# Attention block on one core: the first image's x split between two queues, the shift taken from rstd, and warming from a tile of zeros

## Chip, core and metric

One core of a Trainium2 chip. The metric is the device time of one launch in microseconds, median of the runs. The engines: PE (TensorE), DVE (VectorE), ACT (ScalarE), POOL (GpSimd) and SP (SyncE); SP and ACT each issue DMAs on a hardware queue of their own, POOL on a software queue.

## What is computed

A group norm over 8 groups of 64 channels, then attention with four heads of 128 channels over 1024 positions, a projection and a residual, for 16 images of 512 x 32 x 32, all in float32.

```
xg = x.reshape(b, NUM_GROUPS, -1)
xn = ((xg - mean(xg)) * rsqrt(var(xg) + EPS)).reshape(b, c, h, w)
xn = xn * norm_gamma[:, None, None] + norm_beta[:, None, None]
qkv = einsum('oc,bchw->bohw', qkv_w, xn) + qkv_b[:, None, None]
q, k, v = split(qkv, 3, axis=1)                      # 4 heads each
attn = softmax(einsum('bhnd,bhmd->bhnm', q, k) * dh ** -0.5)
out = einsum('bhnm,bhmd->bhnd', attn, v)
out = einsum('oc,bchw->bohw', proj_w, out) + proj_b[:, None, None]
return x + out
```

## The kernel before

x lies in SBUF as four chunks of 128 channels (partitions) by 1024 positions, `xs[b, c]`. An image goes through the norm, the products for v, q and k (by Strassen-like schemes of seven products or more, so that sums of blocks are formed on DVE first), scores, exponentials, the weighted sum and the projection; the next image's preparation is laid between the scores of the present one. From the first scores on PE goes from one product to the next.

The change touches only the opening of the first image. `open_image` writes out by hand what each engine does there, in program order (`pin`), with priorities (`urgent`) for the scheduler:

- `load_x(0, ...)` asks for each chunk in two column halves of 512 positions, 256 KB each: the left by SP's queue, the right by ACT's. Chunks 0 and 1 (`KC` = 2) come first, then chunks 2 and 3 between the loads of v's weights.
- `stage_v` loads v's weights in blocks `a11`, `a12`, `a21`, `a22` of 256 x 256, each in two pieces `k` of 128 KB, by `load_w`.
- `stats_on_vector(c)` takes mean and variance of chunk 0, then 1, with one BATCH_NORM_STATS2 for a column half and one aggregate. Two products with the averaging matrix `avg` carry them over the channels of a group: `pivot` (L2280, on the first half's mean alone, result `pm`) and `product` (L2300, on the deviations `e` from that pivot). `about` forms `e` from the aggregate and `pm`.
- From the second product ACT forms the variance (`power_on_scalar`), POOL its power -1/2 (`root`: `rstd`), ACT minus the mean (`minus_mean_on_scalar`: `mu`). DVE then makes `sc` = rstd x gamma (`scale`) and `sh` = mu x sc + beta (`shift`), and `quarter` normalises 256 columns at a time, on DVE or ACT. The first product for v (L1065, tile `v_x`) reads such a quarter and a11.
- Chunk 2 goes through DVE and chunk 3 through ACT (`stats_on_scalar`, tile `junk`), then as a pair through the same steps (`lower`).
- `warm(n, jj)` lays n products of `avg` by `avg`, 128 x 128, into tiles `seed`, which nobody reads before they are overwritten. One product in float32 shows as two records of PE.

The program uses eight semaphores for the DMAs of SP and ACT together, DMAHW0 to DMAHW7, in turn. A DMA that takes a semaphore waits until the earlier DMA on it has landed, and the queue behind it waits too.

Of the kernel before, what the change touches and what calls it, by code (L numbers as in the profile page):

```python
# [12 lines left out]
AF = mybir.ActivationFunctionType  # L13
# [3 lines left out]
P = 128  # L17
# [4 lines left out]
HALF = 512  # L22
# [156 lines left out]
KC = 2  # L179
# [56 lines left out]
def fast_path(ctx, tc, x, sources, out, consts, flag, dims):  # L236
# [6 lines left out]
    nc = tc.nc  # L243
    B, C, N, NCC, NH2, NB, GC, SCALE = dims
    gamma, beta, qkv_wT, qk_b, v_b, proj_wT, proj_b = sources
    avg, neghalf, gamma_sb, beta_sb, qkb_sb, vb_sb, projb_sb = consts
# [36 lines left out]
    xs, xb, vs, qs, ks, os_, ob = {}, {}, {}, {}, {}, {}, {}  # L283
# [5 lines left out]
    def load_x(b, chunks=range(NCC)):  # L289
        for c in chunks:  # L290
            if b not in xw:
                xw[b] = every_x
            xs[b, c] = xw[b][:, ts(c, N)]
            for half in range(NH2 if b == 0 else 1):
                i = ts(half, HALF) if b == 0 else ds(0, N)

                eng = nc.gpsimd if b > 0 else nc.scalar if half == 1 else nc.sync
                dma = eng.dma_start(xs[b, c][:, i], x[b, ts(c, P), i])  # L298
                if b > 0:

                    tc.keep_in_program_order(dma)


    home = {
        h: tpool.tile([P, 4, HALF], F32, tag=f"home{h}", name=f"home_{h}") for h in "AB"
    }
    load_x(0, range(KC))
    primer = one.tile([BLK, 1], F32, name="primer")
    for t, src in ((gamma_sb, gamma), (beta_sb, beta)):
        nc.gpsimd.dma_start(t, src)  # L310
    nc.gpsimd.memset(ones, 1.0)
# [260 lines left out]
    def stage_v():  # L572

        beside["v"] = vpool.tile([P, 4, HALF], F32, tag="v", name="wv")
        for i, n in enumerate(("a11", "s1", "a12", "s2")):
            wv[n] = beside["v"][:, i].rearrange("p (k m) -> p k m", m=HC)
        two = [ypool.tile([P, KC, HALF], F32, tag="y", name=f"wv_{i}") for i in range(2)]
        for i, n in enumerate(("a21", "a22", "s4")):
            wv[n] = two[i // 2][:, i % 2].rearrange("p (k m) -> p k m", m=HC)
        beside["spare"] = two[1][:, 1]  # L580
        wv["s3"] = wv["a21"]
        base = 2 * C

        def load_w(n, k, eng):
            r, kk = int(n[1]) - 1, int(n[2]) - 1
            eng.dma_start(wv[n][:, k, :], qkv_wT[ts(KC * kk + k, P), ds(base + r * HC, HC)])

        load_w("a11", 0, nc.sync)
        load_x(0, range(KC, KC + 1))
        load_w("a11", 1, nc.scalar)  # L590
        load_x(0, range(KC + 1, NCC))
        for n in ("a21", "a22", "a12"):
            for k in range(KC):
                load_w(n, k, nc.sync)

    def keep_kept(site, part, eng):

        if site == "v":

            t = rpool.tile([P, 4, HALF], F32, tag=f"r{part}", name=f"kv_tt_{part}")  # L600
            tt = t[:, :2].rearrange("p s (f d) -> p s f d", d=P)
            beside["s4"] = t[:, 2].rearrange("p (f d) -> p f d", d=P)
        else:
            tt = lpool.tile([P, 2, 4, P], F32, tag="tt", name=f"kproj_tt_{part}")
        if part == 0 and site == "proj":
            beside["s4"] = beside["spare"].rearrange("p (f d) -> p f d", d=P)
        if part == 0:
            keep_factors(
                site, ((0, (0, 1)), (1, (0, 1))),
                beside["v"].rearrange("p f (k c d) -> p f k c d", k=KC, c=2),  # L610
                (tt[:, 0], tt[:, 1], beside["s4"]), eng,
            )
            return
        for i, (n, g, o) in enumerate((("s3", 2, 0), ("a22", 2, 1), ("s4", 3, 0))):
            one = slice(i, i + 1)
            keep_factors(
                site, ((g, (o,)),),
                wv[n].rearrange("p k (c d) -> p k c d", c=2).unsqueeze(1),
                (tt[:, 0, one], tt[:, 1, one], beside["s4"][:, one]), eng,
            )  # L620
# [111 lines left out]
    shift = {"now": 0, "next": 0}  # L732
# [1506 lines left out]
    def warm(n, jj):  # L2239

        for _ in range(n):
            i = warmed[jj]
            warmed[jj] += 1
            ins = nc.tensor.matmul(  # L2244
                seeds[jj][:, ts(i % (HALF // P), P)], avg, avg,
                start=(i == 0), stop=True, skip_group_check=True,
            )
            tc.keep_in_program_order(ins)

    def open_image(units):  # L2250


        pin = tc.keep_in_program_order
        mvs[0] = gn.tile([P, NCC, 2], F32, tag="mv", name="mv_0")
        mean, var = ([mvs[0][:, c, i : i + 1] for c in range(NCC)] for i in range(2))
        act, dve = nc.scalar, nc.vector
# [4 lines left out]
        class Chain:  # L2261
# [74 lines left out]

            def minus_mean(self):
                pin(dve.tensor_sub(self.mu, self.mu, self.pms))

            def minus_mean_on_scalar(self):  # L2340
                self.mu, off = self.small("mu"), self.e[:, 0, 0:1]
# [2 lines left out]
                    self.mu, self.pm[0], AF.Identity, scale=-1.0, bias=off  # L2344
                ))

            def scale(self):
                self.sc, self.sh = self.small("sc"), self.small("sh")
                pin(dve.tensor_mul(
                    self.sc, self.rstd, gamma_sb[:, self.c[0] : self.c[-1] + 1]  # L2350
                ))

            def shift(self, i):
                c, o = self.c[i], slice(i, i + 1)
                scaled[0, c] = self.sc, self.sh, i
                pin(dve.scalar_tensor_tensor(
                    self.sh[:, o], self.mu[:, o], self.sc[:, o], beta_sb[:, c : c + 1],
                    ALU.mult, ALU.add,
                ))

        def stats_on_vector(c):
            both = gn.tile([P, NH2 + 1, 6], F32, tag="st", name=f"st_{c}")
            st = both[:, :NH2]
            steps = [
                lambda h=h: pin(dve.bn_stats(st[:, h, :], xs[0, c][:, ts(h, HALF)]))
                for h in range(NH2)
            ]
            steps.append(lambda: pin(
                dve.bn_aggr(mvs[0][:, c, :], st.rearrange("p h s -> p (h s)"))
            ))  # L2370
            return steps, both
# [24 lines left out]
        upper, lower = [Chain(c) for c in range(KC)], Chain(KC, KC + 1)  # L2396

        def urgent(step, *args):
            with tc.high_priority(URGENT):
                return step(*args)  # L2400
# [8 lines left out]
        upper[0].pivot(st[:, 0, 1:2])  # L2409
        run(steps[1:])  # L2410
        urgent(upper[0].about, 0)
        warm(2, 1)
        urgent(upper[0].product)
        warm(1, 1)
        urgent(upper[0].power_on_scalar)
        urgent(upper[0].minus_mean_on_scalar)
        steps, st = stats_on_vector(1)
        run(steps[:1])
        urgent(upper[1].pivot, st[:, 0, 1:2])
        warm(4, 1)  # L2420
        run(steps[1:])
        urgent(upper[1].about, 0)
        urgent(upper[1].product)
# [15 lines left out]
        sum_c()  # L2439
        run(steps[:1])  # L2440
        urgent(upper[1].scale)
        urgent(upper[1].shift, 0)
        quarter(1, 0)
        quarter(1, 1)
        square_c()
# [3 lines left out]
        s1, a21, a22 = wv["s1"], wv["a21"], wv["a22"]  # L2449
# [45 lines left out]
    seeds = [ps_s.tile([P, HALF], F32, tag="s", name=f"seed_{jj}") for jj in range(2)]  # L2495
# [20 lines left out]
    for s in range(steps + 1):  # L2516
        units = []
        if s < steps:
            b, h, j = where(s)
# [12 lines left out]
        for half in range(NH2):  # L2532
# [21 lines left out]
            n = (len(units) + 1) // 2  # L2554
# [158 lines left out]
```

## Time and profile before

| what | value |
|---|---|
| time, median of 3 runs | 3101.13 us (3101.08 to 3101.16) |
| the profiled execution | 3100.82 us, its span 3099.2 us |
| PE busy | 3093.6 us of the span |
| DVE, ACT, POOL busy | 2709.8, 1758.0 and 455.6 us |
| DMA | 647.70 MB, mean 209 GB/s |
| first v product starts | 9.50 us after the span's start |

Times in rows are in microseconds from the span's start. A busy PE is not PE at its peak, since matmul records overlap and their ends are modelled: the pace is read from starts. The change lies in the first 20 us; the views of that stretch are the timeline, the chain of waits and the landings of DMAs.

### The profile page before, as it was taken

Reading aid. Unit: us, or ns where it says so; the run is one execution under the profiler, and the core shown is the slowest. Engines: PE = TensorE matmul, PEld = TensorE weight load, DVE = VectorE, ACT = ScalarE, POOL = GpSimd, SP = SyncE. Lnnn points to the kernel's source line nnn. Section 1 sums busy time; section 2 is a strip of 40 time slices with the busy share of each in tenths; the row PEclk is TensorE's granted clock in tenths of the full one; section 3 lists DMA queues with packets and bytes.
Section 4 is the critical chain, followed back from the end, with each engine's and each line's share of the span. In section 5 each row is a group of like instructions: output and inputs, shape, how many; then the busy total and the mean of one; then the engine's idle time right before and its main releaser. Section 6 shows DMA issues by size and latency. Waiting matters only on the chain.

```text
span 3099.2 us, 39180 instructions
## 1 busy us (share of the span) xinstructions
PE 3093.6 (100%) x12168; PEld 2274.1 (73%) x12168; DVE 2709.8 (87%) x4870; ACT 1758.0 (57%) x3882; POOL 455.6 (15%) x763
## 2 busy tenths in 40 slices
PE   9999999999999999999999999999999999999999
PEld 7567777777777777777777777777777777777775
DVE  8989989889798897988979889898898979989787
ACT  4546556565565655656556565565655656556543
POOL 0131112111111111111111111111111101111010
PEclk9999999999999999999999999999999999999999
DMA  5597686766767667666676666767667566676751
GB/s 180 192 299 262 208 257 213 228 201 200 222 210 216 199 204 218 212 206 205 203 230 204 210 203 200 230 198 214 204 209 221 201 212 207 211 225 194 218 193 42
DMA packets 246228, 647.70 MB, mean 209 GB/s; under 512 B 32816, under 2 KB 77744, under 8 KB 246016
## 3 DMA queue, kind: packets, MB, share of 16 engines
q1 hardware_dynamic: 169248, 380.78, 40.5%
q0 software_dynamic: 63952, 229.91, 21.3%
q10 hardware_dynamic: 12816, 34.48, 3.5%
q8 instruction: 98, 1.61, 0.2%
q14 instruction: 114, 0.93, 0.1%
HBM read 468.08 MB, written 176.96 MB: 208 GB/s over the span
## 4 chain that ended last, share of the span: by engine, by line
PE 100%; DVE 0%; issue 0%
PE s L1787 28%; PE po L1886 28%; PE t_x L1332 16%; PE t_y L1332 8%; PE pp_x L829 6%; PE t_z L1332 4%; PE pp_y L829 3%; PE qk_x L829 2%; PE pp_z L829 1%; PE qk_y L829 1%; PE v_x L1065 0%; PE v_x L829 0%; PE lx L2006 0%; PE seed L2244 0%; PE qk_z L829 0%; PE v_y L829 0%
## 5 line engine op out<-in xcount | busy, mean ns | idle before, releaser
L1886 PE MATMUL po<-p,v 128*128 128x512 f32 x2048 | 1045.4, 592 | 0.0
L1787 PE MATMUL s<-qk,qk 128*128 128x512 f32 x2048 | 1045.2, 592 | 0.0
L1793 ACT ACTIVATE p<-s 128x512 f32<-128x512 f32 x1024 | 610.9, 597 | 510.5 <-PE s L1787 501.2
L1886 PEld LDWEIGHTS po<-p,v 128*128 128x128 f32 x2048 | 616.1, 301 | 375.8 <-issue 259.6
L1808 DVE TENSOR_TENSOR tot<-tot,p 128x1024 f32<-128x1024 f32 (+1 forms) x408 | 472.2, 1158 | 138.8 <-ACT p L1793 134.9
L1787 PEld LDWEIGHTS s<-qk,qk 128*128 128x128 f32 x2048 | 357.6, 189 | 44.5 <-issue 22.7
L1356 DVE TENSOR_TENSOR r<-t_y,t_u 128x342 f32<-128x342 f32 x448 | 217.2, 485 | 157.8 <-PE t_y L1332 122.7
L1452 DVE TENSOR_TENSOR r<-r,r 128x684 f32<-128x684 f32 x308 | 263.7, 864 | 1.6
L1332 PE MATMUL t_x<-home_B,w 128*128 128x171 f32 x1176 | 219.0, 308 | 0.0
L1332 PE MATMUL t_x<-home_A,w 128*128 128x171 f32 x1176 | 219.0, 308 | 0.0
L1332 PEld LDWEIGHTS t_x<-home_B,w 128*128 128x128 f32 x1176 | 188.6, 189 | 35.3 <-issue 23.4
L1332 PEld LDWEIGHTS t_x<-home_A,w 128*128 128x128 f32 x1176 | 188.6, 189 | 35.3 <-issue 23.4
L1292 ACT COPY t_u<-t_x 128x342 f32<-128x342 f32 x224 | 91.8, 410 | 138.7 <-PE t_x L1332 129.8
L1209 DVE TENSOR_TENSOR f<-x 128x684 f32<-128x684 f32 x196 | 168.0, 857 | 0.9
L1142 POOL DMA_DIRECT2D v<-vd x240 | 139.9, 590 | 148.3 <-DMA vd<-vu 58.5
L1332 PEld LDWEIGHTS t_z<-f,w 128*128 128x128 f32 x616 | 104.4, 190 | 60.5 <-issue 40.2
L298 POOL DMA_DIRECT2D x<-in_x x60 | 32.8, 551 | 718.1 <-PE t_x L1332 449.4
L1425 DVE STREAM_TRANSPOSE vu<-vt 128x128 f32<-128x128 f32 x448 | 124.2, 404 | 0.0
L1298 ACT ACTIVATE t_u<-t_x,bias 128x171 f32<-128x171 f32 x224 | 84.2, 403 | 66.3 <-PE t_x L1332 66.3
L1247 POOL DMA_DIRECT2D kept_t<-home_A x112 | 61.4, 549 | 382.0 <-DVE home_A L1240 369.6
L1332 PE MATMUL t_y<-f,w 128*128 128x171 f32 x616 | 116.8, 307 | 0.0
L1332 PE MATMUL t_z<-f,w 128*128 128x171 f32 x616 | 116.7, 308 | 0.0
(421 smaller groups left out, 4991.4 us busy)
## 6 DMA issues: line engine op xcount, KB each, us to landing
w<-kept SPq DMA_DIRECT2D x191, 512.0 KB, 3.9
w<-kept SPq DMA_DIRECT2D x191, 384.0 KB, 3.9
kept_t<-home_A POOLq DMA_DIRECT2D x112, 342.0 KB, 3.7
home_B<-kept_t SPq DMA_DIRECT2D x112, 342.0 KB, 3.4
rinv<-row ACTq DMA_DIRECT2D x63, 512.0 KB, 4.4
x<-in_x POOLq DMA_DIRECT2D x60, 512.0 KB, 6.1
v<-vd POOLq DMA_DIRECT2D x240, 128.0 KB, 4.4
out_y<-y_c POOLq DMA_DIRECT2D x60, 512.0 KB, 3.3
```

Of the source, the lines that this page charges most:

```text
L829: latest["product"] = nc.tensor.matmul(acc[:, ts(i, Q)], have["w"][t][:, i, slot, :], inner(i, bn), start=(first and i == 0), stop=True, s ...
L1142: nc.gpsimd.dma_start(vs[b, pair][ts(q, BLK), half].rearrange("m h (k i) j -> m (h k) (i j)", k=n), rows.rearrange("(k m) (q e) -> q m k e ...
L1209: (eng.tensor_add if op == "+" else eng.tensor_sub)(made[f], of(a), of(c))
L1292: nc.scalar.copy(dst, src)
L1332: latest["product"] = nc.tensor.matmul(acc[:, ts(i, H3)], wts[G, t][:, i, slot, :], moving, start=(start and i == 0), stop=True, skip_grou ...
L1356: out = nc.vector.tensor_add(dst, view(a), view(c))
L1425: nc.vector.transpose(to[:, k], of[:, k])
L1452: (nc.vector.tensor_add if add else nc.vector.tensor_sub)(at(o), a, c)
L1787: latest["score"] = nc.tensor.matmul(sc, ks[b, h][:, ts(j, P)], qs[b, h][:, ts(half, HALF)], start=True, stop=True)
L1793: exps[s] = nc.scalar.activation(ps[s][:, ts(half, HALF)], sc, AF.Exp, scale=SCALE)
L1808: added[b, h, j] = nc.vector.tensor_add(tot[b, h][:, i], tot[b, h][:, i], ps[s][:, i])
L1886: summed = nc.tensor.matmul(po[half], v_block(b, h, j), ps[s][:, i], start=(j == 0), stop=(j == NB - 1),)
```

## The change

- x's chunks 0 and 1: each column half is asked for in two parts of 64 channels, one by SP, one by ACT, so the halves follow each other on both queues. These eight DMAs take all eight semaphores.
- The second piece of a11 moves from ACT's queue to SP's, behind chunk 3's left half; a21 and a22 are asked for piece by piece instead of block by block.
- `still`, 128 x 128 zeros in `home["A"]` (a tile that is used much later), is set by POOL ahead of its first DMAs, and the warming multiplies `still` by itself instead of `avg` by `avg`. Two warming products are dropped: one ahead of chunk 0's `product`, one ahead of chunk 1's.
- The shift of chunk 0 and of the pair of chunks 2 and 3: `mu` is multiplied by gamma (ACT for chunk 0, DVE for the pair) while POOL takes the power, and `sh` = mu x rstd + beta no longer reads `sc`. Chunk 1 keeps `sc`.

```diff
--- before.py
+++ after.py
@@ -293,6 +293,11 @@
             xs[b, c] = xw[b][:, ts(c, N)]
             for half in range(NH2 if b == 0 else 1):
                 i = ts(half, HALF) if b == 0 else ds(0, N)
+                if b == 0 and c < KC:
+                    for part, eng in enumerate((nc.sync, nc.scalar)):
+                        r = ts(part, P // 2)
+                        eng.dma_start(xs[0, c][r, i], x[0, ds(c * P + part * P // 2, P // 2), i])
+                    continue
 
                 eng = nc.gpsimd if b > 0 else nc.scalar if half == 1 else nc.sync
                 dma = eng.dma_start(xs[b, c][:, i], x[b, ts(c, P), i])
@@ -306,6 +311,8 @@
     }
     load_x(0, range(KC))
     primer = one.tile([BLK, 1], F32, name="primer")
+    still = home["A"][:, 0, :P]
+    nc.gpsimd.memset(still, 0.0)
     for t, src in ((gamma_sb, gamma), (beta_sb, beta)):
         nc.gpsimd.dma_start(t, src)
     nc.gpsimd.memset(ones, 1.0)
@@ -587,11 +594,13 @@
 
         load_w("a11", 0, nc.sync)
         load_x(0, range(KC, KC + 1))
-        load_w("a11", 1, nc.scalar)
         load_x(0, range(KC + 1, NCC))
-        for n in ("a21", "a22", "a12"):
-            for k in range(KC):
+        load_w("a11", 1, nc.sync)
+        for k in range(KC):
+            for n in ("a21", "a22"):
                 load_w(n, k, nc.sync)
+        for k in range(KC):
+            load_w("a12", k, nc.sync)
 
     def keep_kept(site, part, eng):
 
@@ -2242,7 +2251,7 @@
             i = warmed[jj]
             warmed[jj] += 1
             ins = nc.tensor.matmul(
-                seeds[jj][:, ts(i % (HALF // P), P)], avg, avg,
+                seeds[jj][:, ts(i % (HALF // P), P)], still, still,
                 start=(i == 0), stop=True, skip_group_check=True,
             )
             tc.keep_in_program_order(ins)
@@ -2336,6 +2345,7 @@
 
             def minus_mean(self):
                 pin(dve.tensor_sub(self.mu, self.mu, self.pms))
+                pin(dve.tensor_mul(self.mu, self.mu, self.gammas()))
 
             def minus_mean_on_scalar(self):
                 self.mu, off = self.small("mu"), self.e[:, 0, 0:1]
@@ -2344,17 +2354,26 @@
                     self.mu, self.pm[0], AF.Identity, scale=-1.0, bias=off
                 ))
 
+            def by_gamma_on_scalar(self):
+                pin(act.activation(
+                    self.mu, self.mu, AF.Identity, scale=self.gammas()
+                ))
+
+            def gammas(self):
+                return gamma_sb[:, self.c[0] : self.c[-1] + 1]
+
             def scale(self):
                 self.sc, self.sh = self.small("sc"), self.small("sh")
                 pin(dve.tensor_mul(
-                    self.sc, self.rstd, gamma_sb[:, self.c[0] : self.c[-1] + 1]
+                    self.sc, self.rstd, self.gammas()
                 ))
 
-            def shift(self, i):
+            def shift(self, i, by=None):
                 c, o = self.c[i], slice(i, i + 1)
                 scaled[0, c] = self.sc, self.sh, i
+                by = self.rstd if by is None else by
                 pin(dve.scalar_tensor_tensor(
-                    self.sh[:, o], self.mu[:, o], self.sc[:, o], beta_sb[:, c : c + 1],
+                    self.sh[:, o], self.mu[:, o], by[:, o], beta_sb[:, c : c + 1],
                     ALU.mult, ALU.add,
                 ))
 
@@ -2409,15 +2428,16 @@
         upper[0].pivot(st[:, 0, 1:2])
         run(steps[1:])
         urgent(upper[0].about, 0)
-        warm(2, 1)
+        warm(1, 1)
         urgent(upper[0].product)
         warm(1, 1)
         urgent(upper[0].power_on_scalar)
         urgent(upper[0].minus_mean_on_scalar)
+        urgent(upper[0].by_gamma_on_scalar)
         steps, st = stats_on_vector(1)
         run(steps[:1])
         urgent(upper[1].pivot, st[:, 0, 1:2])
-        warm(4, 1)
+        warm(3, 1)
         run(steps[1:])
         urgent(upper[1].about, 0)
         urgent(upper[1].product)
@@ -2439,7 +2459,7 @@
         sum_c()
         run(steps[:1])
         urgent(upper[1].scale)
-        urgent(upper[1].shift, 0)
+        urgent(upper[1].shift, 0, upper[1].sc)
         quarter(1, 0)
         quarter(1, 1)
         square_c()
```

SP's queue from its first DMA, before (`wv` without a number holds a11 and later a12, `wv_217` a21 and a22, `st` pieces of the weights for q and k):

```order
L298 DMA x<-in_x 128x512 x2
L586 DMA wv<-in_qkv_wT 128x256
L298 DMA x<-in_x 128x512 x2
L586 DMA wv_217<-in_qkv_wT 128x256 [waits DMAHW0_49]
L586 DMA wv_217<-in_qkv_wT 128x256 [waits DMAHW2_49]
L586 DMA wv_217<-in_qkv_wT 128x256 [waits DMAHW4_49]
L586 DMA wv_217<-in_qkv_wT 128x256 [waits DMAHW5_49]
L586 DMA wv<-in_qkv_wT 128x256 [waits DMAHW6_49]
L586 DMA wv<-in_qkv_wT 128x256 [waits DMAHW7_49]
L460 DMA st_0_231<-in_qkv_wT 128x2x128 [waits DMAHW0_49]
```

and after (`wv` holds a11, `wv_222` a21 and a22):

```order
L299 DMA x<-in_x 64x512 x4
L593 DMA wv<-in_qkv_wT 128x256 [waits DMAHW0_49]
L303 DMA x<-in_x 128x512 [waits DMAHW1_49]
L303 DMA x<-in_x 128x512 [waits DMAHW2_49]
L593 DMA wv<-in_qkv_wT 128x256 [waits DMAHW4_49]
L593 DMA wv_222<-in_qkv_wT 128x256 [waits DMAHW6_49]
L593 DMA wv_222<-in_qkv_wT 128x256 [waits DMAHW7_49]
L593 DMA wv_222<-in_qkv_wT 128x256 [waits DMAHW0_49]
L593 DMA wv_222<-in_qkv_wT 128x256 [waits DMAHW1_49]
L593 DMA wv<-in_qkv_wT 128x256 [waits DMAHW2_49]
L593 DMA wv<-in_qkv_wT 128x256 [waits DMAHW3_49]
L467 DMA st_0_236<-in_qkv_wT 128x2x128 [waits DMAHW4_49]
```

Before, five DMAs go without a wait, a11 among them as the third; now four half-height ones do, and a11, the chunks 2 and 3 and the second a11 each wait for a landing. The first `st` waits for a later DMA's landing.

PE's opening, before (`seed` the warming, `pm` the two products of the statistics):

```order
L2244 MATMUL seed_242<-avg 128x128 [waits DVE_49]
L2244 MATMUL seed_242<-avg 128x128 x8
L2280 MATMUL pm_246<-st_260,avg 128x1 [waits DVE_49]
L2244 MATMUL seed_243<-avg 128x128 x2
L2300 MATMUL pm_246<-e_245,avg 128x2 [waits DVE_49]
L2244 MATMUL seed_243<-avg 128x128
L2280 MATMUL pm_248<-st_282,avg 128x1 [waits DVE_49]
L2244 MATMUL seed_243<-avg 128x128 x4
L2300 MATMUL pm_248<-e_247,avg 128x2 [waits DVE_49]
L2244 MATMUL seed_243<-avg 128x128 x2
L1065 MATMUL v_1_x<-wv,x 128x256 [waits DMAHW4_49,DMAHW1_49,DVE_49]
```

and after:

```order
L2253 MATMUL seed_247<-home_A 128x128 [waits Pool_49]
L2253 MATMUL seed_247<-home_A 128x128 x8
L2289 MATMUL pm_251<-st_265,avg 128x1 [waits DVE_49]
L2253 MATMUL seed_248<-home_A 128x128
L2309 MATMUL pm_251<-e_250,avg 128x2 [waits DVE_49]
L2253 MATMUL seed_248<-home_A 128x128
L2289 MATMUL pm_253<-st_287,avg 128x1 [waits DVE_49]
L2253 MATMUL seed_248<-home_A 128x128 x3
L2309 MATMUL pm_253<-e_252,avg 128x2 [waits DVE_49]
L2253 MATMUL seed_248<-home_A 128x128 x2
L1074 MATMUL v_1_x<-wv,x 128x256 [waits DMAHW1_49,DMAHW0_49,DVE_49]
```

The warming waits for POOL instead of DVE, one product less stands ahead of chunk 0's `pm<-e` and one less ahead of chunk 1's.

DVE from the end of chunk 1's statistics, before (`e` the deviations, `ve` chunk 1's variance):

```order
L2292 TENSOR_TENSOR e_247<-mv_244,pm_248 128x1 [waits DVE_49,PE_49]
L2293 SCALAR_TENSOR_TENSOR e_247<-e_247,mv_244 128x1 [waits DVE_49]
L2349 TENSOR_TENSOR sc_0_298<-rstd_0_277,gamma_sb 128x1 [waits DMASW0_49,Pool_49]
L2356 SCALAR_TENSOR_TENSOR sh_0_299<-mu_0_279,sc_0_298,beta_sb 128x1 [waits DMASW1_49,DVE_49,Activation_49]
L111 TENSOR_SCALAR x<-x,sc_0_298,sh_0_299 128x256 [waits DVE_49]
L2320 SCALAR_TENSOR_TENSOR ve_1_304<-pm_248,d_1_296 128x1 [waits Activation_49]
```

and after:

```order
L2301 TENSOR_TENSOR e_252<-mv_249,pm_253 128x1 [waits DVE_49,PE_49]
L2302 SCALAR_TENSOR_TENSOR e_252<-e_252,mv_249 128x1 [waits DVE_49]
L2367 TENSOR_TENSOR sc_0_302<-rstd_0_281,gamma_sb 128x1 [waits DMASW0_49,Pool_49]
L2375 SCALAR_TENSOR_TENSOR sh_0_303<-mu_0_283,rstd_0_281,beta_sb 128x1 [waits DMASW1_49,Activation_49]
L111 TENSOR_SCALAR x<-x,sc_0_302,sh_0_303 128x256 [waits DVE_49]
L2329 SCALAR_TENSOR_TENSOR ve_1_308<-pm_253,d_1_300 128x1 [waits Activation_49]
```

The order is the same (later a few sums for q and k change places on DVE); `sh` waits for ACT's `mu` and for beta, no longer for the instruction ahead of it.

## The prediction

> **What bounds the kernel now.** I read the page first (which engine, and whether it waits), then the chain of waits in order of time for the first 45 us, then the timeline of the opening, and last the views of the DMAs.
>
> ```profile
> span 3099.2 us, 39180 instructions
> ...
> PE 100%; DVE 0%; issue 0%
> ```
>
> The chain lies on PE for the whole span, so nothing that is hidden beside PE is worth anything. What can move is the time at which PE begins its useful work, and any wait before it is saturated.
>
> ```profile
> 1.64 4.21 PE seed L2244 x18
> ...
> 9.61 2.75 PE v_x L1065 x12
> ...
> 17.53 3.45 PE seed L1065 x16
> 20.98 10.36 PE v_x L1065 x48
> ```
>
> "seed L2244" is the warming, products that nobody reads. The first useful product is v_x at 9.50 (row below). From 17.53 on PE goes at its own pace: 10.36/48 = 0.216 us a record, as 3.45/16. The chain stays on PE between the two as well. So the change is worth what it moves the start at 9.50, if nothing gives it back before 17.53. The timeline of the opening:
>
> ```profile
> 0.98 0.86 SPq L298 DMA_DIRECT2D x<-in_x  x2
> 1.07 0.17 DVE L314 MEMSET avg<- 128x128 f32 x1 [1.07 <-PEq L2701]
> ...
> 1.52 0.70 POOL L310 DMA_DIRECT2D gamma_sb<-in_gamma  x1 [0.84 <-POOLq L2701]
> ...
> 2.77 0.12 POOL L311 MEMSET ones<- 32x1 f32 x1
> 2.80 0.17 POOL L320 MEMSET table<- 128x64 f32 x1
> ...
> 4.61 0.34 ACTq L586 DMA_DIRECT2D wv<-in_qkv_wT  x1
> 4.61 1.29 DVE L2365 BATCH_NORM_STATS2 st<-x 128x6 f32<-128x512 f32 x2 [3.02 <-DMA x<-in_x]
> 5.64 0.42 PE L2280 MATMUL pm<-st,avg 128*128 128x1 f32 x2
> 5.93 0.21 DVE L2369 BATCH_NORM_AGGREGATE mv<-st 128x2 f32<-128x12 f32 x1
> 6.25 0.15 DVE L2292 TENSOR_TENSOR e<-mv,pm 128x1 f32<-128x1 f32 x1
> 6.72 0.38 PE L2300 MATMUL pm<-e,avg 128*128 128x2 f32 x2
> 7.87 0.57 POOL L2327 TENSOR_TENSOR rstd<-ve,neghalf 128x1 f32<-128x1 f32 x1 [4.90 <-ACT e L2342]
> 7.88 0.26 ACT L2343 ACTIVATE mu<-pm,e 128x1 f32<-128x1 f32 x1
> 8.54 0.15 DVE L2349 TENSOR_TENSOR sc<-rstd,gamma_sb 128x1 f32<-128x1 f32 x1
> 8.78 0.22 DVE L2356 SCALAR_TENSOR_TENSOR sh<-mu,sc,beta_sb 128x1 f32<-128x1 f32 x1
> 9.03 0.41 DVE L111 TENSOR_SCALAR x<-x,sc,sh 128x256 f32<-128x256 f32 x1
> 9.09 0.17 ACT L2316 ACTIVATE d<-pm 128x1 f32<-128x1 f32 x1 [0.95 <-PE pm L2300]
> 9.50 2.86 PE L1065 MATMUL v_x<-wv,x 128*128 128x256 f32 x12
> 10.96 1.06 ACT L2379 ACTIVATE junk<-x 128x1024 f32<-128x1024 f32 x1 [0.16 <-DMA x<-in_x]
> 16.10 0.16 DVE L2349 TENSOR_TENSOR sc<-rstd,gamma_sb 128x2 f32<-128x2 f32 x1 [0.21 <-POOL rstd L2327]
> 16.29 0.35 DVE L2356 SCALAR_TENSOR_TENSOR sh<-mu,sc,beta_sb 128x1 f32<-128x1 f32 x2
> ```
>
> DVE idles 3.02 us for the first half of chunk 0; from there a chain without a gap leads to 9.50: statistics, e, the product at 6.72, rstd on POOL, sc, sh, the normalised quarter. It is the path of the opening.
>
> **The landing of x.** The DMA views (landings of the issues at 0.98; packets of ACT's queue from 2.7 to 3.5) and the throughput in half microseconds:
>
> ```profile
> x<-in_x ACTq DMA_DIRECT2D x1, 256.0 KB, 3.8
> x<-in_x SPq DMA_DIRECT2D x1, 256.0 KB, 3.6
> ...
> q10 hardware_dynamic: 55, 0.11, 36.0%
> ...
> 2.00:2.50 0.50, 0.50 (x4) 0.50 (x4) 0.00 (x0) 0.50 (x1) 0.50 (x2) 1.00 0.40 45
> 2.50:3.00 0.50, 0.50 (x4) 0.50 (x4) 0.00 (x0) 0.50 (x1) 0.47 (x3) 1.00 1.00 262
> 3.00:3.50 0.50, 0.50 (x4) 0.50 (x3) 0.00 (x0) 0.39 (x2) 0.00 (x0) 1.00 0.80 299
> 3.50:4.00 0.50, 0.50 (x5) 0.50 (x4) 0.00 (x0) 0.00 (x0) 0.00 (x0) 1.00 1.06 397
> ```
>
> The last number of a row is GB/s. Both column halves of chunk 0 are under way together, 524 KB; the rows add up to 22, 153, 303 and 501 KB by 2.5, 3.0, 3.5 and 4.0, so they are moved at about 4.06, and are seen at 4.58 (SP) and 4.78 (ACT), 0.5 to 0.7 later. If the first half alone goes first, its 262 KB are moved at 3.36 and seen at 3.9 to 4.1. But ACT's queue (q10) moved only 55 packets of 2 KB from 2.7 to 3.5, and its share is now 64: at that pace 3.63, seen at 4.15 to 4.35. The bounds are 3.9 and 4.61 (nothing gained); I take 4.15. The second half is no earlier than now (the same 524 KB, 4.78), so the second BATCH_NORM_STATS2 starts at 4.78 instead of 4.61 + 1.29 - 0.69 = 5.21. **Term 1: aggregate and e come 0.43 earlier**, e at 5.82.
>
> [...]
>
> **The warming.** e also waits for pm (5.64 + 0.42 = 6.06), and pm is behind nine warming products that fill PE from 1.64 on. At present that has 0.15 to spare; with term 1 it would be the later one. The change lets PE start once POOL has zeroed `still`. The duration by POOL's own rows: 0.12 for 1 element, 0.17 for 64, so some 0.23 for 128. Its start is bounded by DVE's first memset after the same barrier, 1.07, and POOL's first work there, 1.52. So PE starts between 1.30 and 1.75. I take 1.35, a little after the early bound, as a memset is all that stands ahead and the lag of the first row may belong to the DMA. pm then ends at 6.06 - 0.29 = 5.77 and e at 5.82 stands. **Term 2: the early start costs nothing and keeps term 1 whole**; at the other bound (1.75) pm ends at 6.17 and e is back at 6.2: term 1 is gone.
>
> The product of 6.72 would come at 6.29. The two rows of single warming records show what the clock is there:
>
> ```profile
> 5.43 0.42 PE L2244 MATMUL seed<-avg 128*128 128x128 f32 x1
> ...
> 6.59 0.28 PE L2244 MATMUL seed<-avg 128*128 128x128 f32 x1
> ```
>
> A record takes 0.42 at 5.43 and 0.28 at 6.59: PE is slow until some time between, though the column of the granted clock reads 1.00 there too. A slow pair with its weights takes up to 0.25 more than the 0.38 at 6.72 (0.42 and a weight load of 0.21 ahead). Bounds 0 and 0.25; I take 0.10, as 6.29 lies in the later half of that stretch. So rstd comes 0.33 earlier.
>
> **The shift.** sh (8.78) follows sc (8.54) by 0.24, as it reads it; two of them that don't read each other are 0.35 - 0.21 = 0.14 apart (row of 16.29). **Term 3: 0.10 earlier.** Its price is a product with gamma on ACT, 0.26 as the row of 7.88; mu is done at 8.14, ACT's next instruction starts at 9.09 after an idle 0.95, so it is covered unless gamma is late. The lower chunks' product with gamma on DVE, 0.15, stands in the wait of 0.21 for POOL (row of 16.10); uncovered it would cost 0.15 there. Two warming products less free PE from work that nobody waits for once the clock is up.
>
> **The queues.** Every DMA of SP and ACT waits for the eighth before it: ACT's wv was issued at 4.61, when chunk 0 landed (0.98 + 3.6). Now four column halves take all eight places, and the first a11 row (asked for at 1.89 now, row below) can go only when the first half has landed, 4.2. Behind it on SP stand x's chunks 2 and 3, the other a11, a21, a22, a12.
>
> ```profile
> wv<-in_qkv_wT SPq DMA_DIRECT2D x1, 128.0 KB, 4.9
> ...
> wv<-in_qkv_wT ACTq DMA_DIRECT2D x1, 128.0 KB, 5.4
> ...
> x<-in_x ACTq DMA_DIRECT2D x1, 256.0 KB, 4.7
> ...
> gamma_sb<-in_gamma POOLq DMA_DIRECT2D x1, 2.0 KB, 5.1
> ```
>
> - a11, first: 4.2 + 4.9 = 9.1 at the worst, needed at 9.05. It was behind two x halves of 256 KB on its queue and beside two more on the other; now the same 1 MB is ahead of it, and asked for when half of that has moved. By the bytes (1049 KB, 303 of them moved by 3.5, at 397 GB/s: 5.4) it lands near 6.3. Cost 0.
> - a11, second: issued when a half of chunk 1 has landed, some 5.4, and 4.7 to 5.4 later it is 10.1 to 10.8; needed by the ninth v_x record, 9.05 + 8 x 0.216 = 10.8. Cost 0, the thinnest cover of all.
> - chunk 3's second half: issued at 6.27 now and landed at 10.97, which ACT's junk waited for (0.16). Issued at 5.4, it should land by 10.1 and be wanted at 10.4.
> - gamma: 1.52 + 5.1 = 6.6, and 0.2 later behind the memset; wanted by ACT at 7.8.
>
> **The sum.** Term 1 less the slow product, 0.43 - 0.10 = 0.33, plus term 3, 0.10: v_x starts 0.43 earlier, at 9.07. What follows to 17.53 hangs on the same engines in the same order and moves with it. Against the profiled execution (3100.82 us, span 3099.2) that is 3100.39; it stands 0.31 below the median of the runs, 3101.13, and from that the time is 3100.7.
>
> **The rivals.**
> [...]
> - *POOL is late.* Its first row after the barrier is at 1.52, and if that lag belongs to POOL and not to the DMA, PE starts at 1.75 and e is where it was. Again term 3 alone, or nothing: 3101.0 to 3101.1.
> - *A weight or a half of x is late.* It decides when a11 lands after 9.07 (first) or 10.8 (second). 0.5 late gives 3101.2.
> - *PE stays slow* (slower than before). The rise came at most 6.59 - 1.64 = 4.95 us after the first warming product. The warming now multiplies zeros, is two products shorter and has a gap ahead of 6.29. If it doesn't count, the rise comes 4.95 us after v_x starts. How much slower PE is then: 18 warming records took 4.21, 0.23 each, where the chain's pace for 256 columns is 0.216, so about half; 2.5 us are lost, plus three products of 0.25 on the way there: 3101.13 - 0.43 + 2.5 + 0.75 = 3103.95. It turns the sign once v_x runs slow for 0.9 us. For it speaks only that no row shows a product of zeros other than avg's, half of which are. [...]
>
> **How the numbers follow.** The forecast has 0.58, the split without effect 0.14, POOL late 0.12, a late transfer 0.11, the slow clock 0.05. The likeliest gives 3100.7, with 3100.4 (first half at 3.9, product not slow: 0.7 gained) to 3100.9 (0.25 for the slow product) of its own. The range reaches over the rivals of 3101.0 to 3101.2 and, as the records are ends of a model, a little beyond the gain: 3100.2 to 3101.3. A measurement of this kernel can tell 0.2% from no change, 6.2 us; all these cases lie within it, the slow clock too. Only something that no row shows could pass it: 0.01 faster, 0.02 slower, 0.97 within.
>
> **What would show it.** The first BATCH_NORM_STATS2 at 4.15 (4.6: term 1 falls); the first seed at 1.35 (1.8: POOL); pm's end at 5.8; sh 0.14 behind sc; v_x at 9.07; v_y's last stretch before PE is saturated at 17.1 instead of 17.53. v_x records 0.43 apart would be the slow clock; a v_x that starts after the quarter's end, a late a11. The forecast is wrong if v_x moves and 17.53 does not: then something between waits for DVE or a DMA that did not move.

## Result and the profile after

| | before | after |
|---|---|---|
| median of the runs, us | 3100.9 (3100.6 to 3101.78, 18 runs) | 3106.61 (3105.16 to 3107.48, 18 runs) |
| profiled execution | 3100.82 | 3106.32 |
| its span | 3099.2 | 3102.6 |
| time outside the span | 1.6 | 3.7 |

The ratio is 1.0018, 95% interval 1.0012 to 1.0025: 5.7 us slower, where 0.4 faster was forecast. Of the profiled execution's 5.5 us, 3.4 lie in the span and 2.1 outside it. First the chain of waits (start, us, what):

```profile
span 3102.6 us, 39191 instructions
...
0.98 0.62 SPq L299
...
1.66 4.56 DMA x<-in_x
...
12.03 3.63 PE v_x L1074 x12
...
18.70 1.99 PE v_y L1074 x8
20.70 3.45 PE seed L1074 x16
24.15 10.36 PE v_x L1074 x48
```

Saturation (seed, 16 records) moved from 17.53 to 20.70, and from there the pace is the old one (10.36 for 48). So 3.2 of the 3.4 us were lost in the opening. (The rows of `seed` at L1074 are useful products that go into the tile of the warming.) The chain now begins with the issue of one DMA and the landing of the next one; the twelve v_x records take 3.63 instead of 2.75. Chosen rows of the timeline of the opening, engine by engine:

```profile
0.98 0.20 POOL L315 MEMSET home_A<- 128x128 f32 x1 [0.29 <-POOLq L2721]
0.98 2.81 SPq L299 DMA_DIRECT2D x<-in_x  x4
0.99 2.51 ACTq L299 DMA_DIRECT2D x<-in_x  x4
1.24 4.21 PE L2253 MATMUL seed<-home_A 128*128 128x128 f32 x18 [1.24 <-POOL home_A L315]
4.38 0.69 DVE L2384 BATCH_NORM_STATS2 st<-x 128x6 f32<-128x512 f32 x1 [2.78 <-DMA x<-in_x]
5.24 0.47 PE L2289 MATMUL pm<-st,avg 128*128 128x1 f32 x2
6.31 0.69 DVE L2384 BATCH_NORM_STATS2 st<-x 128x6 f32<-128x512 f32 x1 [1.24 <-DMA x<-in_x]
7.35 0.16 DVE L2301 TENSOR_TENSOR e<-mv,pm 128x1 f32<-128x1 f32 x1
7.82 0.58 PE L2309 MATMUL pm<-e,avg 128*128 128x2 f32 x2 [1.47 <-DVE e L2302]
9.78 0.16 DVE L2367 TENSOR_TENSOR sc<-rstd,gamma_sb 128x1 f32<-128x1 f32 x1
9.86 0.22 DVE L2375 SCALAR_TENSOR_TENSOR sh<-mu,rstd,beta_sb 128x1 f32<-128x1 f32 x1
10.12 0.41 DVE L111 TENSOR_SCALAR x<-x,sc,sh 128x256 f32<-128x256 f32 x1
11.82 3.84 PE L1074 MATMUL v_x<-wv,x 128*128 128x256 f32 x12
```

Four issues took SP 2.81, 0.70 each, where two took 0.86. The first half's statistics start 0.23 earlier than before, the second half's 1.10 later (6.31 against 5.21), with an idle 1.24 ahead of them on DVE. PE, which had no gap here before, waits 1.47 for e. The first quarter is normalised at 10.53, but v_x starts only at 11.82: PE works off its own warming products first, at the slow pace (a record every 0.21 us, and v_x's first ones 0.42 apart). The throughput in half microseconds (GB/s is the last number) shows why the halves drift apart:

```profile
3.00:3.50 0.50, 0.50 (x4) 0.50 (x4) 0.00 (x0) 0.00 (x0) 0.01 (x1) 1.00 0.94 327
3.50:4.00 0.50, 0.50 (x5) 0.50 (x4) 0.00 (x0) 0.47 (x1) 0.00 (x0) 1.00 1.10 242
4.00:4.50 0.50, 0.50 (x4) 0.50 (x4) 0.12 (x1) 0.50 (x1) 0.00 (x0) 1.00 1.18 207
4.50:5.00 0.50, 0.50 (x4) 0.50 (x4) 0.50 (x1) 0.49 (x2) 0.00 (x0) 1.00 0.78 153
```

Before, the row of 3.5 to 4.0 had 397, and the next two were

```profile
4.00:4.50 0.50, 0.50 (x4) 0.50 (x4) 0.00 (x0) 0.00 (x0) 0.00 (x0) 1.00 1.09 365
4.50:5.00 0.50, 0.50 (x4) 0.50 (x3) 0.39 (x1) 0.00 (x0) 0.00 (x0) 1.00 0.95 344
```

The DMA engines' share, next to the last, is about as high as then: they are busy, and move little more than half. Last, the DMA view of the stretch from 3103 to 3110, after the last instruction; in the kernel before, the last packet of instructions comes at 3097.5, inside the span.

```profile
DMA packets 2, 0.02 MB, mean 2 GB/s; under 512 B 0, under 2 KB 0, under 8 KB 0
...
q14 instruction: 2, 0.02, 0.7%
```

Two packets of instructions are fetched, at 3104.18 and 3106.37 of the span's clock (the execution took 3106.32, but that time does not begin with the span): a second loss, with nothing of the opening in it.

So three losses are to be priced: the late half, the slow v_x, the end. In the expectations from "POOL padded by 3" on, theory C is that the 2.1 us at the end hang on the length of POOL's program.

### The profile page after: what moved, and what is told of

Read it like the earlier page. It is cut to its first block, busy times and chain, and to the rows that moved or that the text cites. A ratio compares the mean times of both kernels' runs of the same rounds, so it can differ in the third digit from the quotient of the medians.

```text
span 3102.6 us, 39191 instructions
## 1 busy us (share of the span) xinstructions
PE 3095.8 (100%) x12164; PEld 2276.3 (73%) x12164; DVE 2709.7 (87%) x4871; ACT 1756.6 (57%) x3883; POOL 454.4 (15%) x764
## 4 chain that ended last, share of the span: by engine, by line
PE 100%; DMA 0%; DVE 0%; SPq 0%; issue 0%; DVEq 0%
PE s L1796 28%; PE po L1895 28%; PE t_x L1341 16%; PE t_y L1341 8%; PE pp_x L838 6%; PE t_z L1341 4%; PE pp_y L838 3%; PE qk_x L838 2%; PE pp_z L838 1%; PE qk_y L838 1%; PE v_x L1074 0%; PE v_x L838 0%; PE lx L2015 0%; PE qk_z L838 0%; PE v_y L838 0%; PE qk_o L838 0%
```

## The experiments

Twelve kernels, ten runs each. "Outside" is the profiled time less its span; POOL is the number of its instructions in the trace; the clock column gives, in us of the span, where the trace's record of PE's granted clock goes to full (+) or half (-). Ahead of the first such record the rows of the windows read 1.00 whatever PE's pace is (in the changed kernel also from 11.80 to 14.00, where v_x's records are 0.42 apart), so the slow stretch at the start can't be seen in them.

| kernel | median (range), us | ratio to before, 95% | outside | POOL | clock |
|---|---|---|---|---|---|
| before | 3100.9 (3100.51 to 3103.91, all groups) | | 1.6 | 1360 | +6.44 |
| after | 3106.61 | 1.0012 to 1.0025 | 3.7 | 1363 | +14.01 |
| whole halves | 3102.03 (3100.66 to 3104.61) | 0.9994 to 1.0013 | 1.7 | 1361 | +6.17 |
| split alone | 3102.71 (3102.19 to 3104.07) | 0.9997 to 1.0016 | 1.7 | 1362 | +5.28 |
| warm by avg | 3104.53 (3103.83 to 3105.46) | 1.0002 to 1.0021 | 1.8 | 1362 | +4.79 -8.21 +15.03 |
| column quarters | 3102.56 (3101.05 to 3103.66) | 0.9996 to 1.0015 | 1.6 | 1360 | +14.16 |
| two warm fewer | 3100.93 (3100.63 to 3102.37) | 0.9991 to 1.0010 | 1.6 | 1360 | +5.94 -9.35 +12.77 |
| quarters, full warm | 3101.40 (3100.41 to 3102.33) | 0.9993 to 1.0012 | 1.6 | 1360 | +7.25 |
| POOL padded by 3 | 3103.04 (3102.76 to 3103.30) | 0.9997 to 1.0016 | 3.9 | 1363 | +5.48 |
| after, dense warm | 3104.59 (3103.69 to 3107.92) | 1.0005 to 1.0024 | 3.8 | 1363 | +4.16 |
| whole, full warm | 3100.72 (3100.47 to 3101.86) | 0.9991 to 1.0010 | 1.7 | 1361 | +5.27 |
| chunk 0 quarters | 3103.41 (3101.30 to 3105.33) | 0.9998 to 1.0017 | 1.7 | 1361 | +5.29 -8.70 +12.11 |
| POOL padded by 24 | 3101.21 (3100.96 to 3101.58) | 0.9991 to 1.0010 | 1.7 | 1386 | +7.09 |
| after, POOL padded | 3104.27 (3102.27 to 3104.90) | 1.0001 to 1.0020 | 1.7 | 1387 | +5.50 -8.92 +15.74 |

Before was run beside each group (medians 3100.78 to 3100.98). Most intervals hold 1 and some ranges overlap, so what follows rests on medians of ten runs and on the profiles beside them.

**Whole halves**: the change without the split.

```diff
-                if b == 0 and c < KC:
-                    for part, eng in enumerate((nc.sync, nc.scalar)):
-                        r = ts(part, P // 2)
-                        eng.dma_start(xs[0, c][r, i], x[0, ds(c * P + part * P // 2, P // 2), i])
-                    continue
```

> The change with x's chunks 0 and 1 asked for as before (128-row column halves, left by SP, right by ACT); the zeros, the gamma edit and the order of the weights stay. Theory A (the 64-row transfers are slow, and the gap that they leave on PE holds PE's slow stretch open): the second statistics of chunk 0 start near 5.2 again, PE has no gap ahead of v_x, v_x starts at 9.3 to 9.5 at the fast pace, span 3098.9 to 3099.3. Theory B (products of zeros don't bring PE up): v_x's first records stay 0.43 apart, span 3101 or more. The time outside the span is 1.6 before and 3.7 in the change, which neither explains; a third idea, that it hangs on where the instruction streams end, lets it be either here.

3102.03, single runs from 3100.66 to 3104.61. In the profiled one the statistics come at 4.69 without a gap and the clock rises at 6.17, although PE multiplies zeros. Most of the loss is gone with the split, 2.1 of it at the end (1.7 outside the span instead of 3.7); the spread, wider than that of before, is not.

**Split alone**: the kernel before with only those lines added.

> The kernel before with the 64-row transfers alone (warming by avg, shift from the scale, the weights' old order). Theory A: the second half of chunk 0 lands near 6.2, e at 7.3, PE stands idle more than 1 us ahead of it, v_x starts slow at 11.5 to 12, span 3102 to 3103.5. Theory B: e late, but PE fast by 7.5 and v_x at 10.6 at the fast pace, span 3100.2 to 3100.6.

3102.71, +1.8 with every warming product kept. The timeline:

```profile
0.98 2.80 SPq L299 DMA_DIRECT2D x<-in_x  x4
...
4.48 0.70 DVE L2370 BATCH_NORM_STATS2 st<-x 128x6 f32<-128x512 f32 x1 [2.90 <-DMA x<-in_x]
5.69 0.69 DVE L2370 BATCH_NORM_STATS2 st<-x 128x6 f32<-128x512 f32 x1 [0.52 <-DMA x<-in_x]
...
7.20 0.38 PE L2305 MATMUL pm<-e,avg 128*128 128x2 f32 x2 [0.90 <-DVE e L2298]
...
7.86 0.33 ACTq L303 DMA_DIRECT2D x<-in_x  x1
8.24 0.17 ACT L2314 ACTIVATE d<-pm 128x1 f32<-128x1 f32 x1 [3.23 <-PE pm L2285]
...
12.54 1.06 ACT L2384 ACTIVATE junk<-x 128x1024 f32<-128x1024 f32 x1 [0.77 <-DMA x<-in_x]
```

The slow issue and the late second half are the split's own. The clock held in the profiled run, and saturation came at 19.08, 1.55 later than before. But the product with e starts only 0.48 later (7.20 against 6.72); the rest is lost behind ACT's queue. In this kernel the second a11 still stands on ACT's queue, and the issue of chunk 3's right half behind it had to wait until 7.86 for a landing (6.27 before). ACT took up the variance (`d`) only behind that issue, 0.66 after the product's end. In the kernel before it was 0.04 (7.10 and 7.14). (The profile puts the wait of `d` down to chunk 1's pivot; before, `d` ran ahead of that pivot, 7.14 against 7.32, so the issue is the likelier cause, though not shown to be.) Chunk 3 then landed late, and `junk`, on the chain of waits, stood 0.77 for it. The changed kernel, with a11 moved to SP, shows neither wait.

**Warm by avg**: the changed kernel, its warming fed by `avg`, without POOL's memset.

```diff
-    still = home["A"][:, 0, :P]
-    nc.gpsimd.memset(still, 0.0)
...
-                seeds[jj][:, ts(i % (HALF // P), P)], still, still,
+                seeds[jj][:, ts(i % (HALF // P), P)], avg, avg,
```

> The whole change but for the zeros: the warming multiplies avg by avg again and waits for DVE. Theory A: as the change, span 3102 to 3103.5, v_x's first records slow. Theory B: PE fast ahead of v_x, span 3100.6 or less.

PE is slow here too, so zeros are not the cause: without the end, the two kernels are 0.2 apart (3104.53 less 1.8 and 3106.61 less 3.7). The stretches of 3.4 and 3.2 us (PE's busy time and records first, the granted clock third from the end):

```profile
4.80:8.20 3.40, 1.92 (x15) 1.54 (x14) 2.47 (x7) 0.74 (x6) 0.00 (x0) 1.00 1.03 281
8.30:11.50 3.20, 3.20 (x15) 3.15 (x15) 2.42 (x10) 1.77 (x8) 1.33 (x3) 0.50 0.97 314
```

The clock rose at 4.79; in the 3.4 us behind that PE was busy for 1.92 (it waited 1.21 for e), and at 8.21, 3.42 after the rise, the clock fell to half, for 6.82 us, until 15.03. The end of this kernel costs 1.8, not 3.7.

**Column quarters**: the same order, waits and number of DMAs, cut by columns, so that each has 128 rows.

```diff
-                        r = ts(part, P // 2)
-                        eng.dma_start(xs[0, c][r, i], x[0, ds(c * P + part * P // 2, P // 2), i])
+                        q = ts(2 * half + part, Q)
+                        eng.dma_start(xs[0, c][:, q], x[0, ts(c, P), q])
```

> The change with each column half cut by columns instead of channels: two transfers of 128 rows by 256 columns, one by SP, one by ACT, so order, sizes, queues and waits are those of the change. Theory A, if the height of 64 is what is slow: issues of 0.4 us, the first half seen by 4.3 and the second by 4.9, e at 5.9, v_x fast at 9.1 to 9.3, span 3098.7 to 3099. If instead the order (eight transfers with everything else behind their landings) is what is slow: the second half near 6.2 again and a span of 3102 or more.

```profile
0.98 1.81 SPq L299 DMA_DIRECT2D x<-in_x  x4
4.01 1.44 DVE L2384 BATCH_NORM_STATS2 st<-x 128x6 f32<-128x512 f32 x2 [2.42 <-DMA x<-in_x]
...
6.65 1.40 DVE L2384 BATCH_NORM_STATS2 st<-x 128x6 f32<-128x512 f32 x2 [0.45 <-DMA x<-in_x]
```

With 128 rows an issue takes 0.45, chunk 0 lands at 4.0, and its second half causes no gap: what made the second half late is the height of 64 rows, not the order. (The throughput from 3.5 to 5.0 is below that of before here too, 220 to 303 GB/s against 344 to 397, so that drop is not the height's alone.) Yet the time is 3102.56: PE was slow until 14.16.

**Two warm fewer**: the kernel before with the changed kernel's counts.

```diff
-        warm(2, 1)
+        warm(1, 1)
...
-        warm(4, 1)
+        warm(3, 1)
```

> The kernel before with nothing changed but two warming products less (one instead of two ahead of the product with e, three instead of four ahead of the second). [...] Rival, the two products carry the rise by themselves: rise near 14 in most runs, 3102.5 to 3104. Rival, the count does not matter at all: 3100.9, spread as before.

3100.93: the median does not move, but three of ten runs are at 3101.8 to 3102.4. The profiled one (3102.35) lost the clock at 9.35. In the kernel before, two products fewer are a risk, not a loss at the median. (In the changed kernel without the 64 rows they are one, as the two pairs of runs with full warming below show.)

**After, dense warm**: the changed kernel with counts 9, 5, 2, 4, 2, which put the two products back and leave 0.56 of the gap ahead of e.

```diff
-        warm(1, 1)
+        warm(5, 1)
         urgent(upper[0].product)
-        warm(1, 1)
+        warm(2, 1)
...
-        warm(3, 1)
+        warm(4, 1)
```

> The changed kernel as it is, 64-row halves and all, with the warming counts 9, 5, 2, 4, 2 instead of 9, 1, 1, 3, 2, so that PE has products to stream while e is late (5.2 to 7.8). [...] Rival, PE is slow in the changed kernel for another reason than the gap (zeros, the late half itself): rise near 14 still, 3106.6 or a little more.

```profile
10.13 2.65 PE v_x L1074 x12
...
17.99 3.45 PE seed L1074 x16
```

3104.59, 2.0 less than the changed kernel, by warming products alone, though two of the ten runs were no better than it (3106.5 and 3107.9). In the profiled one v_x has its full pace (2.65), and saturation is 2.7 earlier; the second half was seen at 5.7 there, 0.6 of these 2.7. The medians price the slow clock at 2.0, give or take some tenths; gap and dropped products are not told apart by this run.

**Quarters, full warm**: column quarters with the counts of before (9, 2, 1, 4, 2).

```diff
-        warm(1, 1)
+        warm(2, 1)
...
-        warm(3, 1)
+        warm(4, 1)
```

> The changed kernel with column quarters instead of 64-row halves (as the run of column quarters) and with the two warming products put back (9, 2, 1, 4, 2). [...] Rival, the earlier start or the zeros keep PE slow, or e's being earlier leaves gaps that two products do not fill: as column quarters, 3102.6, v_x at 10.3 or later.

3101.40, 1.2 less than column quarters by the two products alone. PE is quick (the clock rises at 7.25), but v_x starts at 9.58, where it was 9.50. In the timeline e is 0.50 earlier than before (5.94 against 6.44), and sc 0.13 later (8.67):

```profile
5.94 0.22 DVE L2302 SCALAR_TENSOR_TENSOR e<-e,mv 128x1 f32<-128x1 f32 x1
6.58 1.42 DVE L2384 BATCH_NORM_STATS2 st<-x 128x6 f32<-128x512 f32 x2 [0.41 <-DMA x<-in_x]
...
8.54 0.22 DVE L2302 SCALAR_TENSOR_TENSOR e<-e,mv 128x1 f32<-128x1 f32 x1
8.67 0.15 DVE L2367 TENSOR_TENSOR sc<-rstd,gamma_sb 128x1 f32<-128x1 f32 x1
```

On DVE, sc stands behind all of chunk 1's statistics and e, and chunk 1 did not come earlier.

**Chunk 0 quarters**: as that, but chunk 1 in whole halves, to bring chunk 1 forward too.

```diff
-                if b == 0 and c < KC:
+                if b == c == 0:
```

> As the run of column quarters with full warming, but only chunk 0 in quarters; chunk 1 in whole halves as before. Chunk 0's statistics at 4.0 as there (4.61 before); chunk 1's first half, asked for at 1.9, should be seen by 6.3 instead of 6.58 or 7.28, since the queues issue one DMA less ahead of it. The scale stands behind chunk 1's second e on DVE, so what counts is chunk 1: sc at 8.3 to 8.5 (8.54 before, 8.67 there), v_x at 9.2 to 9.4; 3100.4 to 3100.8. Rival, chunk 1 is late here too (first half at 6.6 or later): sc no earlier than 8.6 and 3101 or more. Outside the span 1.6.

```profile
5.81 0.22 DVE L2302 SCALAR_TENSOR_TENSOR e<-e,mv 128x1 f32<-128x1 f32 x1
...
7.24 0.57 POOL L2336 TENSOR_TENSOR rstd<-ve,neghalf 128x1 f32<-128x1 f32 x1 [4.24 <-ACT e L2352]
...
7.74 1.29 DVE L2384 BATCH_NORM_STATS2 st<-x 128x6 f32<-128x512 f32 x2 [1.71 <-DMA x<-in_x]
...
9.71 0.15 DVE L2367 TENSOR_TENSOR sc<-rstd,gamma_sb 128x1 f32<-128x1 f32 x1
```

A miss: 3103.41. Chunk 0 is all that was hoped for, e 0.63 earlier and rstd at 7.24 instead of 7.87; but chunk 1 is seen at 7.74, DVE idles 1.71, and sc waits until 9.71. PE idled too, 1.69 ahead of the product at 8.49, and its clock fell at 8.70.

**POOL padded by 3**: the kernel before, with three idle memsets.

```diff
-    nc.gpsimd.memset(table, 0.0)
+    for _ in range(4):
+        nc.gpsimd.memset(table, 0.0)
```

> The kernel before with POOL's memset of the table repeated three times more at its place in the opening (2.80, POOL then idles until 7.87): POOL executes 1363 recorded instructions instead of 1360, as in the changed kernel. Theory C, the 2.1 us outside the span hang on the length of POOL's program (1360, 1360 and 1361 instructions: 1.6 to 1.7 us outside; 1362 twice: one refill more at the end; 1363: two refills after the last instruction and 3.7 us): 3103.0, two instruction packets after the last instruction, span unchanged at 3099.2. Rival, the refill hangs on another engine's program or on where the run stands in time: 3100.9, 1.6 us outside.

```profile
span 3099.2 us, 39183 instructions
...
q14 instruction: 2, 0.02, 1.4%
```

3103.04 (3103.0 expected), the span unchanged, and two packets of instructions fetched after the last instruction (the second line, from the DMA view of 3100 to 3104). Three instructions that do nothing cost 2.1 us.

**POOL padded by 24**: the same, more often.

```diff
-    for _ in range(4):
+    for _ in range(25):
```

> The kernel before with the memset of the table repeated 24 times more (the earlier padding had 3), 1384 recorded instructions on POOL. Theory C as a boundary that a few instructions cross: once crossed, 21 more add nothing, 3.7 to 3.9 us outside the span, 3103.0 to 3103.3. Rival, the end grows with every instruction: clearly over 3103.5. Rival, it hangs on the place within a block and comes and goes: 1.6 outside, 3100.9. The memsets (24 x 0.1 to 0.17, 2.4 to 4.1 us from 2.9 on) end ahead of 7.87, so the span stays 3099.2.

3101.21 and 1.7 outside: the loss is gone again (the 0.2 left is about what POOL's rstd came later behind the memsets, 8.06 against 7.87). So it neither grows with the number of POOL's instructions nor stays (1363 have it, 1386 don't): of the three cases only the last agrees, that it comes and goes.

**After, POOL padded**: the changed kernel with 23 idle memsets more.

```diff
-    nc.gpsimd.memset(table, 0.0)
+    for _ in range(24):
+        nc.gpsimd.memset(table, 0.0)
```

> The changed kernel with the memset of the table repeated 23 times more: POOL executes 1386 recorded instructions, as in the longer padding of the kernel before (1.7 us outside the span there), instead of 1363. Theory C, the 2.1 us outside the span hang on where POOL's program ends within its blocks of instructions: 1.6 to 1.8 outside, no instruction packet after the last instruction, 3104.5 although POOL does more. The memsets end by 8.2, ahead of POOL's rstd at 9.18, so the opening stays as it was (3102.6 span, 20.7 at saturation). Rival, in the changed kernel something else adds the 2.1 us (the instructions of SP, ACT or PE): 3.7 outside and 3106.6.

3104.27, against 3106.61, by adding work. With 1387 instructions on POOL 1.7 lie outside, with 1363 it was 3.7; theory C, so corrected, holds in the changed kernel too.

**Whole, full warm**: the run of whole halves, with the counts of before.

```diff
-        warm(1, 1)
+        warm(2, 1)
...
-        warm(3, 1)
+        warm(4, 1)
```

> The change without the 64-row split (whole halves of 256 KB, one a queue) and with the warming counts of before (9, 2, 1, 4, 2); zeros, early start, the order of the weights and the shift's edit stay. [...] Theory C: POOL's program 1361, 1.6 to 1.7 us outside the span. Rival, the spread of the run of whole halves came from the order of the weights or the zeros: 3102.0 again.

3100.72 against 3100.98 for before in the same group, interval 0.9991 to 1.0010: the best of all, and not to be told from before. Saturation came at 17.35 instead of 17.53; one run of ten was above 3101.6. Against whole halves (3102.03) the two products alone are worth 1.3.

**The account.** The end costs 2.1 (3.7 outside the span, less 1.6; 2.2 and 2.3 by the medians of the two paddings). It is there in every run: the 38 runs of the three kernels with 1363 instructions on POOL have 3.7 to 4.1 outside the span, all others on record 1.5 to 1.9. The slow clock, from the gap and the two dropped products together, costs 2.0 (dense warm). Of 5.7, 1.6 are left for the late half and for what of the slow clock the denser warming does not cure; no run measures them apart. The rows of the profiled run agree: the product with e starts 1.10 later than before (7.82 against 6.72), which is the late half; saturation comes 3.17 later, and the other 2.1 arise while PE is never idle but slow, in the warming products and in v_x. That the split alone cost 1.8 is no second measurement of the late half, since in its profile only 0.48 of 1.55 came with that half: that the two figures are alike is luck.

One profile shows the clock of one run only, but each run's mean granted clock is on record. In the twelve experiments' traces it is 0.999 where the clock fell again in the opening and 1.000 where it did not. It is 0.999 in 12 of 18 runs of the changed kernel, 8 of 10 with warm by avg, 3 of 10 with the split alone, 2 of 10 with dense warming, and in none of the 100 runs of before that stood beside the experiments.

## Why the prediction was wrong, point by point

- **Term 1, the landing: failed.** "The second half is no earlier than now (the same 524 KB, 4.78)" was used as if it were no later. Its statistics start at 6.31 (5.6 to 5.9 in the four other traces with 64 rows, against 5.21 before: late in all of them). It stands second on both queues and a 64-row transfer takes 0.70 to issue instead of 0.43, so it is asked for at 1.66 instead of 0.98; and the engines then move 153 to 242 GB/s instead of 344 to 397. The first half at 4.38 lies inside the bounds, 0.23 worse than taken. No row showed a 64-row transfer; a split without effect had 0.14 and no price above zero. No run shows one without effect: with nothing but the split added (split alone) the second half's statistics start 0.48 later than before and the time is 1.8 longer, and in the changed kernel the product with e starts 1.10 later. A late half of x had 0.11, for half a microsecond.
- **From e to v_x: failed too, unseen.** "So rstd comes 0.33 earlier" was carried through to v_x. But DVE's order has chunk 1's statistics, aggregate and e ahead of sc. In the kernel before, rstd ended at 8.44 and the row below ran until 8.62; and sc starts 0.14 behind that row's start, as closely as in the two runs with quarters (0.13 and 0.14), where rstd was ready earlier; so chunk 0 alone could win nothing there. The two runs with quarters showed it: e 0.50 and 0.63 earlier, sc 0.13 and 1.17 later.

```profile
8.40 0.22 DVE L2293 SCALAR_TENSOR_TENSOR e<-e,mv 128x1 f32<-128x1 f32 x1
```

- **Term 2, the early start: right.** POOL's memset at 0.98, the first seed at 1.24 (1.35), pm's end at 5.71 (5.77). With term 1 gone it kept nothing; and as the warming starts and ends earlier, it leaves more of the wait for e uncovered.
- **PE stays slow: the right rival with a wrong chance.** 0.05 for 3103.95; it happened, and with the end's cost taken away the changed kernel has 3104.27. Of its three causes, zeros fell (warm by avg). Two products fewer, which the prediction put at nothing ("work that nobody waits for once the clock is up"), only add risk in the kernel before, but cost 1.2 to 1.3 at the median in the changed kernel with whole halves or column quarters. Filling the gap and putting the two products back took 2.0 of the 3.6 away that are not the end's (after, dense warm). I took the gap as the forecast had it, a few tenths; a late half makes it 1.47. That two rivals feed each other, late transfer and slow clock, was not in the chances.
- **Term 3, the shift: right.** sh starts 0.08 behind sc (0.14 forecast).
- **The queues: right, as far as they were tried.** v_x did not wait for a weight, but it also came 2.3 later than before, so the thin covers were not put to the test. ACT's product with gamma, 0.29 long, was done ahead of sh.
- **What lies outside the span: not considered.** The sum was made "Against the profiled execution (3100.82 us, span 3099.2)", as if the 1.6 between them were constant. It grew to 3.7, and those 2.1 are more than a third of the loss.
- The condition named for being wrong, v_x moving without 17.53, was not the way it went: both moved, the wrong way.
- The yardstick of 6.2 us, below which nothing can be told from no change, was too wide: the interval of 1.0012 to 1.0025 leaves no change out at 5.7 us.

## What to carry to other kernels

A transfer that is cut must be priced again: give "no earlier" a "no later" before using it, and try a cut that keeps all 128 rows (here 0.45 us an issue instead of 0.70). An earlier input is worth only what the engine that takes it can use (here e came 0.50 earlier and sc 0.13 later), so read the order of the instructions up to the one that waits, for every input ahead of it. And split a small difference into span and remainder first: here 2.1 us of it were the program's end, which three idle instructions brought and 23 took away.

## What the runs showed of the hardware

- In the four traces with three changes of PE's granted clock the steps between them are 3.41 to 3.42 us or twice that: 3.42 and 6.82 (warm by avg, and after, POOL padded), 3.41 and 3.42 (two warm fewer), 3.41 and 3.41 (chunk 0 quarters). The first rise differs from run to run (4.16 to 7.25, or at 14), so one profile says little of the other runs; the mean granted clock of every run says more.
- How busy PE must be for the clock to rise or to hold is not settled. After the rise, stretches of 3.41 us in which PE was busy for 1.72 (chunk 0 quarters), 1.93 (warm by avg) and 2.09 us (after, POOL padded) ended in a fall; but one with 2.80 did (first row, two warm fewer) and one with 2.52 did not (second row, split alone). Nor did the clock rise in column quarters after 3.41 busy of 3.41 (third row; it rose at 14.16), by the profile's reckoning, in which the short products and their weights count in full.

```profile
5.94:9.35 3.41, 2.80 (x20) 2.33 (x21) 2.93 (x12) 1.10 (x7) 0.57 (x1) 1.00 1.03 367
```
```profile
5.28:8.69 3.41, 2.52 (x21) 2.24 (x21) 2.60 (x7) 0.41 (x3) 0.00 (x0) 1.00 1.06 297
```
```profile
7.34:10.75 3.41, 3.41 (x16) 3.35 (x16) 2.66 (x10) 1.79 (x9) 1.14 (x3) 1.00 1.02 338
```

- The three kernels with 1363 instructions on POOL have 3.7 to 3.9 us outside the span; those with 1360 to 1362 and with 1386 or 1387 have 1.6 to 1.8. Two packets of instructions are fetched after the last instruction in the three traces with 3.7 to 3.9, none in before and one in warm by avg (1.8 outside). What number of instructions brings the two packets was not tried further.
- Why 64 rows are slow to issue and to move stays open; the runs show only that at equal order and number of DMAs an issue takes 0.70 with 64 rows and 0.45 with 128, and that the second half is late with 64 rows alone (an idle 1.24 on DVE ahead of its statistics in the changed kernel, 0.52 in split alone, none in column quarters).
